# Linear attention and a routed expert layer: the experts' first product with the weights as its stationary side

## Chip, cores and metric

One core of a Trainium2 chip runs the whole kernel in one launch. The metric is the device time in microseconds of that core. Everything is float32.

## The reference, cut to what matters

The input is 2 x 2048 = 4096 tokens of 512 features. The first half of the layer is a linear attention with 16 query heads and 4 key heads of 128, between two normalisations, added back to its input. The second half, which the change is in, is a mixture of 32 experts, of which each token takes 8:

```python
logits = x @ wg.T
scores = softmax(logits)
weights, idx = top_k(scores, 8);  weights = weights / sum(weights)
# the tokens sorted by expert; per expert's group of rows:
g = xs @ w1[e]          # 512 -> 192
u = xs @ v1[e]          # 512 -> 192
h = silu(g) * u
ys = h @ w2[e]          # 192 -> 512
out[t] += ys * weight   # added up over the 8 experts of a token
x + layernorm(out)
```

## The kernel before, in words

**Routing.** While the attention runs, `route_tile` computes the scores of 128 tokens, the place of each token in its experts' lists, and writes token number and weight to `list_d` in DRAM with eight indirect DMAs of GpSimd (L203). `plan_round` (L254 on) cuts the lists into blocks of 128 tokens of one expert. Its tables give, for every block, the token numbers (`tid`), their weights (`wt`), and the expert to load, with a mark where the same buffer still holds that expert's weights (`keep`, L338), in which case the loads are skipped.

**Pairs of blocks.** Two blocks are worked on together, s = 0 and 1. A first round of 24 pairs (L731 to L734) takes blocks that are full after seven of the eight attention tiles; it starts while the last routing work is still going on. A second round of up to 120 pairs follows, cut into parts of 104, 8, 2, 2, 2 and 2 pairs (`PARTS`, L77); each part but the first stands behind a branch on the number of pairs that there really are (L770). In this input 138 pairs run in all: 24, then 104, 8 and 2.

**`prepare`** (L666) takes a pair's buffers `r` (one of three sets, `NR`) and for each of its blocks has SyncE load the expert's first weights (`w1t`, L674: 128 partitions x 4 slices x 384 columns, gate and up side by side) and second weights (`w2t`, L675 and L676), has GpSimd gather the 128 tokens (`xg`, L679), transposes them on TensorE in four 128x128 pieces (`px`, L685), and copies the result to `xgT` on VectorE (L687).

**`run_pair`** (L691) does the two products. For each block, TensorE takes the transposed tokens as the stationary side and streams 384 weight columns against them, in four accumulating steps (`pgu`, L698): the result has tokens on partitions. ScalarE applies silu to the gate half (L701) and VectorE multiplies it with the up half into `hh` (L702), with the 192 features reordered. The two blocks' 2 x 192 features are then transposed in three 128x128 pieces (`ph`, L710) and copied to `hT` (L712): piece 0 holds 128 features of block 0, piece 2 holds 128 of block 1, piece 1 has the remaining 64 of block 0 on partitions 0 to 63 and those of block 1 on 64 to 127. The second product has a full-row part for each block (L715) and a 64-row part for each (L719), which accumulate in `py`. ScalarE scales by the routing weight (L723), and GpSimd adds the rows to `acc_d` in DRAM by an indirect DMA (L724).

**Order.** The Tile framework schedules the instructions of each engine from the program's order and its dependencies; SyncE's order alone is as written. Pools say how many buffers there are: 4 of `xg`, 6 of `xgT`, 2 PSUM tiles each of `px`, `pgu` and `py`, one of `ph`. In the second round the program prepares pair i+1 ahead of running pair i (`second_round`, L752). The pair that stands first behind a branch is prepared in the part ahead of it, into tiles of its own (`ahead`).

A last loop adds up the two accumulators, normalises, and adds the attention's output.

Of the kernel before, what the change touches and what calls it, by code (L numbers as in the profile page):

```python
# [8 lines left out]
F32 = mybir.dt.float32  # L9
I32 = mybir.dt.int32  # L10
U32 = mybir.dt.uint32
AF = mybir.ActivationFunctionType
# [5 lines left out]
P = 128  # L18
# [5 lines left out]
def linear_attention_then_moe(  # L24
# [15 lines left out]
    nc = tc.nc  # L40

    NT, HID = x.shape
# [6 lines left out]
    C = HID // P  # L49
    E = wgT.shape[1]  # L50
    K = 8
    F2 = wgu.shape[1] // C
    F = F2 // 2
    FC = w2r.shape[1] // HID
    FR = F - P
    NR = 3
    NTILE = NT // P
# [15 lines left out]
    NP2 = (NB - N1 + 1) // 2  # L73
# [2 lines left out]

    PARTS = [(NT * K // BS - N1) // 2, 8, 2, 2, 2, 2]  # L77
    assert sum(PARTS) == NP2


    dram = ctx.enter_context(tc.tile_pool(name="dram", bufs=1, space=DRAM))

    x1_d = dram.tile([NT, HID], F32, name="x1_d")
    xn_d = dram.tile([NT + P, HID], F32, name="xn_d")
# [7 lines left out]
    ident = const.tile([P, P], F32, name="ident")  # L92
# [554 lines left out]
    with ExitStack() as mctx:  # L647
        plan = mctx.enter_context(tc.tile_pool(name="plan", bufs=1))
        x1_sb = plan.tile([P, NTILE, HID], F32, name="x1_sb")
# [3 lines left out]
        hp = pairs.enter_context(tc.tile_pool(name="hp", bufs=3))  # L653
        ps_a = pairs.enter_context(tc.tile_pool(name="ps_a", bufs=2, space=PSUM))


        def weights(shape, name):
            return [[wp.tile(shape, F32, name=f"{name}{s}{r}") for r in range(NR)] for s in range(2)]

        w1b = weights([P, C * F2], "w1t")  # L660
        w2b = weights([P, 2, HID], "w2t")

        w2v = w2r.rearrange("r (c h) -> (r c) h", c=FC)
        pairs.enter_context(tc.manual_schedule(engines={mybir.EngineType.SP}))

        def prepare(r, cols, tid, wt, load, xsrc, into=None):  # L666

            xgTs = []
            for s, c0 in enumerate(cols):
                w1t, w2t = w1b[s][r], w2b[s][r]  # L670
                ld = nc.sync.value_load(load[:, c0 : c0 + 1], min_val=0, max_val=2 * E - 1)
                ex = ld & (E - 1)
                skip = {"cond": ld < E, "bounds_check": "skip_entire_dma"}
                nc.sync.dma_start(w1t, wgu[bass.ds(ex * P, P), :], **skip)  # L674
                nc.sync.dma_start(w2t[:, 0, :], w2v[bass.ds(ex * F + s * FR, P), :], **skip)  # L675
                nc.sync.dma_start(w2t[s * FR : (s + 1) * FR, 1, :],  # L676
                                  w2v[bass.ds(ex * F + (1 - s) * P, FR), :], **skip)
                xg = xg_p.tile([P, HID], F32, tag="xg", name="xg")
                nc.gpsimd.indirect_dma_start(  # L679
                    out=xg, out_offset=None, in_=xsrc,  # L680
                    in_offset=bass.IndirectOffsetOnAxis(ap=tid[:, c0 : c0 + 1], axis=0),
                )
                px = ps_a.tile([P, C, P], F32, tag="xt", name="px")
                for c in range(C):
                    nc.tensor.transpose(px[:, c, :], xg[:, c * P : (c + 1) * P], ident)  # L685
                xgT = into[s] if into else hp.tile([P, C, P], F32, tag="xgT", name="xgT", bufs=6)
                nc.vector.tensor_copy(xgT, px)  # L687
                xgTs.append(xgT)
            return xgTs

        def run_pair(r, cols, tid, wt, load, xgTs):  # L691

            hh = hp.tile([P, 2, F], F32, tag="hh", name="hh")
            for s, xgT in enumerate(xgTs):
                w1t = w1b[s][r]
                pgu = ps_a.tile([P, F2], F32, tag="gu", name="pgu")
                for c in range(C):
                    nc.tensor.matmul(pgu, xgT[:, c, :], w1t[:, c * F2 : (c + 1) * F2],  # L698
                                     start=(c == 0), stop=(c == C - 1))
                hs = hp.tile([P, F], F32, tag="hs", name="hs")  # L700
                nc.scalar.activation(hs, pgu[:, :F], AF.Silu)  # L701
                nc.vector.tensor_mul(  # L702
                    hh[:, s, :].rearrange("p (k c) -> p c k", c=FC),
                    hs.rearrange("p (c k) -> p c k", c=FC),
                    pgu[:, F:].rearrange("p (c k) -> p c k", c=FC),
                )
            hf = hh.rearrange("p s f -> p (s f)")
            ph = ps_a.tile([P, 3, P], F32, tag="ht", name="ph", bufs=1)
            for c in range(3):
                nc.tensor.transpose(ph[:, c, :], hf[:, c * P : (c + 1) * P], ident)  # L710
            hT = hp.tile([P, 3, P], F32, tag="hT", name="hT")
            nc.vector.tensor_copy(hT, ph)  # L712
            py = [ps_a.tile([P, HID], F32, tag="y", name=f"py{s}") for s in range(2)]
            for s in range(2):
                nc.tensor.matmul(py[s], hT[:, 2 * s, :], w2b[s][r][:, 0, :],  # L715
                                 start=True, stop=False)
            for s in range(2):
                rows = slice(s * FR, (s + 1) * FR)
                mm = nc.tensor.matmul(py[s], hT[rows, 1, :], w2b[s][r][rows, 1, :],  # L719
                                      start=False, stop=True)  # L720
            for s, c0 in enumerate(cols):
                ysb = hp.tile([P, HID], F32, tag="ysb", name="ysb")
                nc.scalar.activation(ysb, py[s], AF.Copy, scale=wt[:, c0 : c0 + 1])  # L723
                sc = nc.gpsimd.indirect_dma_start(  # L724
                    out=acc_d[s][:, :],
                    out_offset=bass.IndirectOffsetOnAxis(ap=tid[:, c0 : c0 + 1], axis=0),
                    in_=ysb, in_offset=None, compute_op=ALU.add,
                )
            return mm, sc

        done = []  # L731
        for i in range(NP1):
            pair = (i % NR, (i, NP1 + i), *(a[:, 0, :] for a in round1[:3]))
            done.append(run_pair(*pair, prepare(*pair, xn_d[: SNAP * TB, :])))  # L734
# [6 lines left out]
        np2 = plan.tile([P, 1], I32, name="np2")  # L741
        nc.vector.tensor_copy(np2, round2[3])
        np2 = nc.values_load(np2[:1, :], min_val=0, max_val=NP2)

        def pair2(i):
            g, jj = divmod(i, GP2)
            return (NP1 + i) % NR, (jj, GP2 + jj), *(a[:, g, :] for a in round2[:3])


        ahead = [[plan.tile([P, C, P], F32, name=f"ahead{k}{s}") for s in range(2)] for k in range(2)]  # L750

        def second_round(k, ready):  # L752
            i0, n = sum(PARTS[:k]), PARTS[k]
            for i in range(i0, i0 + n):
                if i % 3 == 0 and i // 3 < NTILE:
                    t = i // 3
                    nc.sync.dma_start(x1_sb[:, t, :], x1_d[t * P : (t + 1) * P, :])
                now, ready = ready, None
                if i + 1 < i0 + n:
                    ready = prepare(*pair2(i + 1), xn_d[:, :])  # L760
                elif i + 1 < NP2:
                    ready = prepare(*pair2(i + 1), xn_d[:, :], ahead[k % 2])
                run_pair(*pair2(i), now)
            return ready

        with ExitStack() as asked:
            ready = prepare(*pair2(0), xn_d[:, :])
            for k in range(len(PARTS)):
                if k:
                    asked.enter_context(tc.If(np2 > sum(PARTS[:k])))  # L770
                ready = second_round(k, ready)
        pairs.close()


# [1 line left out]
        for i in range(0, NTILE, 2):  # L776
            rows = slice(i * P, (i + 2) * P)
# [60 lines left out]
```

## Time and profile before

| | |
|---|---|
| median of 3 runs | 2855.76 us (2848.94 to 2856.44) |
| the profiled execution's own time | 2853.38 us |
| its span, first to last instruction | 2851.6 us |
| mean granted TensorE clock | 0.969 |
| first of the experts' products to the last | 1341 to 2763 us |
| DMA moved over the span | 400.35 MB |

A profile is one execution. Each group of instructions is named by its line, engine, operation and tiles, with count, busy time, mean duration, and the idle time of its engine just ahead of it with what ended that. PEld is TensorE's loading of the stationary side, which runs beside its products. A float32 product leaves two records, a transposition one. Matmul durations overlap those of their neighbours, so what one costs is read from the distance of the starts. The slices of section 2 are a fortieth of the span each, 71 us; TensorE is busy for nine tenths or more of nearly all of those between the start and the final stage:

```profile
PE   8999999998999999998769899999999999999850
DVE  5334544546533536564412222222222222222217
POOL 1100223122320122223455455555555555554426
PEclk9999999999999999999889999999999999999985
```

### The profile page before, as it was taken

The page shows a single profiled execution, that of the slowest core. Times are in us where ns is not written, and L with a number is a line of the kernel's source. Part 1 is how long each engine was busy: PE and PEld are TensorE (multiplying, and loading weights), DVE is VectorE, ACT ScalarE, POOL GpSimd, SP SyncE. Part 2 cuts the span into 40 slices and gives each one's busy share as a digit, 9 for nine tenths or more (in the row PEclk, how much of TensorE's full clock was granted, in tenths as well). Part 3 has the DMA queues.
Part 4 walks back from the last instruction along what each step waited for, and adds up shares of the span by engine and source line. Part 5 has one row for each costly group of instructions (what it writes and reads, how often), then busy time and mean ns, then how long its engine had stood idle before and what let it go on. Part 6 is the DMA issues. An engine that isn't in the chain of part 4 may idle for free. (4 is left out here: it accounts for less than half of the span.)

```text
span 2851.6 us, 29678 instructions
## 1 busy us (share of the span) xinstructions
PE 2642.3 (93%) x8451; PEld 1308.6 (46%) x8451; DVE 1062.9 (37%) x2434; ACT 674.9 (24%) x1208; POOL 1062.5 (37%) x893
## 2 busy tenths in 40 slices
PE   8999999998999999998769899999999999999850
PEld 3434444444444444444435455555555555555420
DVE  5334544546533536564412222222222222222217
ACT  4331222313431313121212112121212121212114
POOL 1100223122320122223455455555555555554426
PEclk9999999999999999999889999999999999999985
DMA  3291211212111212123657899989787988676548
GB/s 112 85 327 52 72 52 52 67 52 68 38 56 45 71 34 71 49 75 113 163 113 165 218 268 253 278 201 253 164 215 158 316 195 199 135 193 122 106 89 319
DMA packets 179450, 400.35 MB, mean 140 GB/s; under 512 B 29445, under 2 KB 30470, under 8 KB 178770
## 3 DMA queue, kind: packets, MB, share of 16 engines
q0 software_dynamic: 70304, 145.84, 25.3%
q1 hardware_dynamic: 101602, 237.55, 25.0%
q10 hardware_dynamic: 7376, 15.02, 1.5%
q8 instruction: 70, 1.15, 0.2%
q14 instruction: 98, 0.80, 0.1%
HBM read 491.63 MB, written 116.66 MB: 213 GB/s over the span
## 5 line engine op out<-in xcount | busy, mean ns | idle before, releaser
L698 PE MATMUL pgu<-w1t,xgT 128*128 128x384 f32 x2176 | 767.6, 496 | 3.6 <-issue 2.5
L724 POOL DMA_INDIRECT acc_d<-ysb,tid x276 | 441.5, 1600 | 499.9 <-ACT ysb L723 385.7
L203 POOL DMA_INDIRECT list_d<-tw,pi x256 | 252.6, 987 | 972.0 <-DVE pi L201 556.1
L698 PEld LDWEIGHTS pgu<-w1t,xgT 128*128 128x128 f32 x2176 | 392.9, 191 | 324.3 <-issue 108.6
L552 PE MATMUL pq<-xlT,wq_sb 128*128 128x512 f32 x1024 | 462.0, 597 | 1.2 <-DVE sq L559 1.2
L584 PE MATMUL acc<-m,sq 128*128 128x512 f32 x1024 | 463.0, 597 | 0.0
L702 DVE TENSOR_TENSOR hh<-hs,pgu 128x192 f32<-128x192 f32 x276 | 97.5, 355 | 976.4 <-ACT hs L701 836.2
L723 ACT ACTIVATE ysb<-py,wt 128x512 f32<-128x512 f32 x276 | 176.6, 684 | 786.6 <-PE py L719 738.4
L679 POOL DMA_INDIRECT xg<-xn_d,tid x278 | 276.5, 995 | 119.8 <-PE px L685 68.0
L552 PEld LDWEIGHTS pq<-xlT,wq_sb 128*128 128x128 f32 x1024 | 190.2, 190 | 240.4 <-issue 229.6
L584 PEld LDWEIGHTS acc<-m,sq 128*128 128x128 f32 x1024 | 189.1, 190 | 239.6 <-issue 239.1
L715 PE MATMUL py<-w2t,hT 128*128 128x512 f32 x552 | 266.4, 605 | 2.1 <-issue 2.1
L555 ACT ACTIVATE qe<-pq,nbq_sb 128x512 f32<-128x512 f32 x128 | 87.7, 685 | 512.9 <-PE pq L552 512.9
L559 DVE SCALAR_TENSOR_TENSOR sq<-pq,bq_sb,qe 128x512 f32<-128x512 f32 x128 | 95.7, 748 | 286.4 <-ACT qe L556 286.2
L687 DVE COPY xgT<-px 128x512 f32<-128x512 f32 x272 | 185.5, 683 | 39.9 <-PE px L685 37.4
L685 PE MATMUL px<-ident,xg 128*128 128x128 f32 x1112 | 173.0, 281 | 26.2 <-DMA xg<-xn_d,tid 16.8
L701 ACT ACTIVATE hs<-pgu 128x192 f32<-128x192 f32 x276 | 90.4, 330 | 353.9 <-PE pgu L698 317.1
L685 PEld LDWEIGHTS px<-ident,xg 128*128 128x128 f32 x1112 | 135.1, 145 | 52.8 <-issue 32.4
L715 PEld LDWEIGHTS py<-w2t,hT 128*128 128x128 f32 x552 | 107.5, 196 | 108.8 <-issue 74.2
L719 PE MATMUL py<-w2t,hT 64*128 64x512 f32 x552 | 157.3, 642 | 0.0
L710 PE MATMUL ph<-ident,hh 128*128 128x128 f32 x414 | 100.1, 297 | 46.9 <-DVE hh L702 46.9
L469 PE MATMUL pk<-wk_sb,xlT 128*128 128x512 f32 x256 | 119.6, 607 | 0.0
(188 smaller groups left out, 1868.0 us busy)
## 6 DMA issues: line engine op xcount, KB each, us to landing
w1t<-in_wgu_dram SPq DMA_DIRECT2D x278, 768.0 KB
w2t<-in_w2r_dram SPq DMA_DIRECT2D x278, 256.0 KB
w2t<-in_w2r_dram SPq DMA_DIRECT2D x278, 128.0 KB
nb<-nr_d SPq DMA_DIRECT2D x128, 256.0 KB
acc_d<-zero SPq DMA_DIRECT2D x6, 2048.0 KB
xb<-in_x_dram SPq DMA_DIRECT2D x32, 256.0 KB
xr<-in_x_dram SPq DMA_DIRECT2D x32, 256.0 KB
wo<-in_woT_dram SPq DMA_DIRECT2D x32, 256.0 KB
```

The source lines that it names most:

```text
L203: nc.gpsimd.indirect_dma_start(out=list_d[:, :], out_offset=bass.IndirectOffsetOnAxis(ap=pi[:, k : k + 1], axis=0), in_=tw[:, k, :], in_of ...
L469: nc.tensor.matmul(pk, xlT[:, c, :], wk_sb[:, c, :], start=(c == 0), stop=(c == C - 1))
L552: nc.tensor.matmul(pq, wq_sb[:, c, h * P : (h + 1) * P], xlT[:, c, :], start=(c == 0), stop=(c == C - 1))
L584: nc.tensor.matmul(pa[s], a[:, s * P : (s + 1) * P], ms[h], start=(h == 0), stop=(h == H - 1))
L679: nc.gpsimd.indirect_dma_start(out=xg, out_offset=None, in_=xsrc, in_offset=bass.IndirectOffsetOnAxis(ap=tid[:, c0 : c0 + 1], axis=0),)
L685: nc.tensor.transpose(px[:, c, :], xg[:, c * P : (c + 1) * P], ident)
L687: nc.vector.tensor_copy(xgT, px)
L698: nc.tensor.matmul(pgu, xgT[:, c, :], w1t[:, c * F2 : (c + 1) * F2], start=(c == 0), stop=(c == C - 1))
L715: nc.tensor.matmul(py[s], hT[:, 2 * s, :], w2b[s][r][:, 0, :], start=True, stop=False)
L719: mm = nc.tensor.matmul(py[s], hT[rows, 1, :], w2b[s][r][rows, 1, :], start=False, stop=True)
L723: nc.scalar.activation(ysb, py[s], AF.Copy, scale=wt[:, c0 : c0 + 1])
L724: sc = nc.gpsimd.indirect_dma_start(out=acc_d[s][:, :], out_offset=bass.IndirectOffsetOnAxis(ap=tid[:, c0 : c0 + 1], axis=0), in_=ysb, in_ ...
```

## The change

Four things change, all in the experts' part.

- The first product is turned round. The stationary side is a slice of 128 weight columns, the moving side the transposed tokens: three slices of four accumulating steps, each over 128 tokens. The result has features on partitions, in three slices of one PSUM tile: gate 0 to 127; gate 128 to 191 with up 0 to 63; up 64 to 191.
- Silu is applied to the first two of these slices (256 columns), and four VectorE products a block, of 64, 64, 32 and 32 partitions, write the features straight into `hT`. `hh`, the transposition `ph` and its copy are gone; `pgu` has three PSUM tiles in place of two.
- The features in `hT` stand in another order, so the rows of `w2` are loaded in that order: each of the two loads reads two runs of rows (`two_runs`).
- The second round prepares pairs two ahead of the one that runs, across branches too, as long as a part has more than two pairs. `AHEAD` is 2.

The second product, the scaling and the scatter are as before in the program's text; so is the first round's loop.

```diff
+    AHEAD = 2
...
+        def two_runs(rows, n, p, dc):
+
+            width = FC * HID
+            return bass.AP(rows.tensor, rows.offset, [[p * width + dc * HID, 2], [width, n], [1, HID]],
+                           runtime_checks=rows.runtime_checks)
...
-                nc.sync.dma_start(w2t[:, 0, :], w2v[bass.ds(ex * F + s * FR, P), :], **skip)
-                nc.sync.dma_start(w2t[s * FR : (s + 1) * FR, 1, :],
-                                  w2v[bass.ds(ex * F + (1 - s) * P, FR), :], **skip)
+                first, second = (w2r[bass.ds(ex * FW, FW), c * HID : (c + 1) * HID] for c in range(FC))
+                nc.sync.dma_start(w2t[:, 0, :], two_runs(first, FR, FW - FR, 1), **skip)
+                nc.sync.dma_start(w2t[s * FR : (s + 1) * FR, 1, :], two_runs(second, FR // 2, FR, -1),
+                                  **skip)
...
-            hh = hp.tile([P, 2, F], F32, tag="hh", name="hh")
             for s, xgT in enumerate(xgTs):
-                pgu = ps_a.tile([P, F2], F32, tag="gu", name="pgu")
-                for c in range(C):
-                    nc.tensor.matmul(pgu, xgT[:, c, :], w1t[:, c * F2 : (c + 1) * F2],
-                                     start=(c == 0), stop=(c == C - 1))
-                hs = hp.tile([P, F], F32, tag="hs", name="hs")
-                nc.scalar.activation(hs, pgu[:, :F], AF.Silu)
-                nc.vector.tensor_mul(
-                    hh[:, s, :].rearrange("p (k c) -> p c k", c=FC),
...
-            ph = ps_a.tile([P, 3, P], F32, tag="ht", name="ph", bufs=1)
-            for c in range(3):
-                nc.tensor.transpose(ph[:, c, :], hf[:, c * P : (c + 1) * P], ident)
-            nc.vector.tensor_copy(hT, ph)
+                pgu = ps_a.tile([P, 3, P], F32, tag="gu", name="pgu", bufs=3)
+                w1t = w1b[s][r].rearrange("p (c k f) -> p c k f", c=C, k=3)
+                for k in range(3):
+                    for c in range(C):
+                        nc.tensor.matmul(pgu[:, k, :], w1t[:, c, k, :], xgT[:, c, :],
+                                         start=(c == 0), stop=(c == C - 1))
+                hs = hp.tile([P, 2, P], F32, tag="hs", name="hs")
+                nc.scalar.activation(hs, pgu[:, :2, :], AF.Silu)
+                main, q, t = hT[:, 2 * s, :], FR // 2, s * FR
+                nc.vector.tensor_mul(main[:FR], hs[:FR, 0, :], pgu[FR:, 1, :])
+                nc.vector.tensor_mul(main[FR:], hs[:FR, 1, :], pgu[FR:, 2, :])
+                nc.vector.tensor_mul(hT[t : t + q, 1, :], hs[FR + q :, 0, :], pgu[q:FR, 2, :])
+                nc.vector.tensor_mul(hT[t + q : t + FR, 1, :], hs[FR : FR + q, 0, :], pgu[:q, 2, :])
...
+                prepare_to(i0, i0 + AHEAD)
+                for i in range(i0, i0 + n):
...
+                    prepare_to(i, min(i + AHEAD, i0 + n - 1) + 1)
+                    if i + AHEAD >= i0 + n and n > AHEAD:
+                        j = i + AHEAD
+                        ready[j] = prepare(*pair2(j), xn_d[:, :], ahead[j - i0 - n])
+                    run_pair(*pair2(i), ready.pop(i))
```

More of the change, by code (lines that the diff above doesn't have):

```diff
@@ L78, in linear_attention_then_moe @@
     assert sum(PARTS) == NP2
+    AHEAD = 2
+    assert min(PARTS) >= AHEAD
     dram = ctx.enter_context(tc.tile_pool(name="dram", bufs=1, space=DRAM))
@@ L661, in linear_attention_then_moe @@
         w2b = weights([P, 2, HID], "w2t")
-        w2v = w2r.rearrange("r (c h) -> (r c) h", c=FC)
+        FW = F // FC
+        assert FC == 2 and F == 3 * FR
+        def two_runs(rows, n, p, dc):
+            width = FC * HID
+            return bass.AP(rows.tensor, rows.offset, [[p * width + dc * HID, 2], [width, n], [1, HID]],
+                           runtime_checks=rows.runtime_checks)
         pairs.enter_context(tc.manual_schedule(engines={mybir.EngineType.SP}))
@@ L691, in run_pair @@
         def run_pair(r, cols, tid, wt, load, xgTs):
-            hh = hp.tile([P, 2, F], F32, tag="hh", name="hh")
+            hT = hp.tile([P, 3, P], F32, tag="hT", name="hT")
             for s, xgT in enumerate(xgTs):
-                w1t = w1b[s][r]
-                pgu = ps_a.tile([P, F2], F32, tag="gu", name="pgu")
-                for c in range(C):
-                    nc.tensor.matmul(pgu, xgT[:, c, :], w1t[:, c * F2 : (c + 1) * F2],
-                                     start=(c == 0), stop=(c == C - 1))
-                hs = hp.tile([P, F], F32, tag="hs", name="hs")
-                nc.scalar.activation(hs, pgu[:, :F], AF.Silu)
-                nc.vector.tensor_mul(
-                    hh[:, s, :].rearrange("p (k c) -> p c k", c=FC),
[L704 to L707, printed above, removed]
-            ph = ps_a.tile([P, 3, P], F32, tag="ht", name="ph", bufs=1)
-            for c in range(3):
-                nc.tensor.transpose(ph[:, c, :], hf[:, c * P : (c + 1) * P], ident)
-            hT = hp.tile([P, 3, P], F32, tag="hT", name="hT")
-            nc.vector.tensor_copy(hT, ph)
+                pgu = ps_a.tile([P, 3, P], F32, tag="gu", name="pgu", bufs=3)
[11 more added lines that the diff above has]
+                nc.vector.tensor_mul(hT[t + q : t + FR, 1, :], hs[FR : FR + q, 0, :], pgu[:q, 2, :])
             py = [ps_a.tile([P, HID], F32, tag="y", name=f"py{s}") for s in range(2)]
@@ L747, in pair2, with prepare_to @@
             return (NP1 + i) % NR, (jj, GP2 + jj), *(a[:, g, :] for a in round2[:3])
[L750 to L764, printed above, removed]
+        ahead = [[plan.tile([P, C, P], F32, name=f"ahead{k}{s}") for s in range(2)] for k in range(AHEAD)]
+        ready = {}
+        def prepare_to(i, n):
+            for j in range(i, n):
+                if j not in ready:
+                    ready[j] = prepare(*pair2(j), xn_d[:, :])
         with ExitStack() as asked:
-            ready = prepare(*pair2(0), xn_d[:, :])
-            for k in range(len(PARTS)):
+            for k, n in enumerate(PARTS):
+                i0 = sum(PARTS[:k])
                 if k:
-                    asked.enter_context(tc.If(np2 > sum(PARTS[:k])))
-                ready = second_round(k, ready)
+                    asked.enter_context(tc.If(np2 > i0))
+                prepare_to(i0, i0 + AHEAD)
+                for i in range(i0, i0 + n):
+                    if i % 3 == 0 and i // 3 < NTILE:
+                        t = i // 3
+                        nc.sync.dma_start(x1_sb[:, t, :], x1_d[t * P : (t + 1) * P, :])
+                    prepare_to(i, min(i + AHEAD, i0 + n - 1) + 1)
[3 more added lines that the diff above has]
+                    run_pair(*pair2(i), ready.pop(i))
         pairs.close()
```

## Prediction

> **What bounds the kernel now.** I read the page first: busy shares, the 40 slices, the costliest groups. Then the busy time by stretch, and last TensorE's timeline through one pair of blocks. The change touches only the experts' part, 1341 to 2770 us. In its middle TensorE never rests:
>
> ```profile
> PE 2642.3 (93%) x8451; PEld 1308.6 (46%) x8451; DVE 1062.9 (37%) x2434; ACT 674.9 (24%) x1208; POOL 1062.5 (37%) x893
> ...
> L698 PE MATMUL pgu<-w1t,xgT 128*128 128x384 f32 x2176 | 767.6, 496 | 3.6 <-issue 2.5
> ...
> L710 PE MATMUL ph<-ident,hh 128*128 128x128 f32 x414 | 100.1, 297 | 46.9 <-DVE hh L702 46.9
> ```
> ```profile
> 1663.00:2641.00 978.00, 976.24 (x3596) 529.45 (x3595) 245.99 (x513) 198.38 (x412) 529.24 (x406) 1.00 0.83 208
> ```
>
> The columns of the last line: stretch, its length, busy us of PE, PEld, DVE, ACT, POOL, granted clock, DMA share, GB/s. PE is busy for 976 of 978 us at full clock; every other engine is at 54% or less. So here time is what TensorE issues, and a cost is the distance between starts, not a duration: durations overlap. One pair, TensorE alone (start, duration to the end of the last one, count):
>
> ```profile
> 2019.31 0.27 PE L710 MATMUL ph<-ident,hh 128*128 128x128 f32 x1
> 2019.42 0.93 PE L685 MATMUL px<-ident,xg 128*128 128x128 f32 x7
> 2020.29 0.44 PE L710 MATMUL ph<-ident,hh 128*128 128x128 f32 x2
> 2020.56 0.27 PE L685 MATMUL px<-ident,xg 128*128 128x128 f32 x1
> 2020.67 1.46 PE L698 MATMUL pgu<-w1t,xgT 128*128 128x384 f32 x4
> 2021.96 1.88 PE L715 MATMUL py<-w2t,hT 128*128 128x512 f32 x4
> 2023.77 1.13 PE L719 MATMUL py<-w2t,hT 64*128 64x512 f32 x4
> 2024.83 4.14 PE L698 MATMUL pgu<-w1t,xgT 128*128 128x384 f32 x12
> 2028.81 0.27 PE L710 MATMUL ph<-ident,hh 128*128 128x128 f32 x1
> ```
>
> A float32 product is recorded as two passes, a transposition as one. The pair's period is 2028.81-2019.31 = 9.50 us. By start differences: ph 0.11+0.27 = 0.38; px 0.98, of which 0.10 is the wait for hh (seven at 0.11 are 0.77, not 0.87); pgu 1.29+3.98 = 5.27 (16 passes of 0.323, one of them 0.10 longer, just after the 64-row products); py's full-row part 1.81 (4 x 0.43, and 0.09 before what follows); py's 64-row part 1.06. Sum 9.50. Periods repeat to 0.01 us over a hundred pairs.
>
> **The change, part by part.**
>
> *Features' transposition removed.* ph goes: 3 x 0.11 = 0.33, the hh wait 0.10, and the 0.05 by which ph's last pair exceeds two passes: -0.48 us a pair. Its copy to hT (0.56 us of DVE) goes as well, off the path.
>
> *First product turned round.* 16 passes over 384 columns become 48 over 128, each with its own stationary tile. The trace has such runs, in the key state:
>
> ```profile
> 802.78 0.83 PE L519 MATMUL pc<-ones,sks 128*128 128x128 f32 x6
> ...
> 803.45 3.89 PE L525 MATMUL pg<-gc,wv_sb 128*128 128x128 f32 x32
> ```
>
> L519: (0.83-0.275)/5 = 0.111 us a pass. L525: (3.89-0.275)/31 = 0.117, with two short waits for PSUM in it; starts inside its groups are 0.112 apart. Three at 0.112 are 0.335 against 0.323, so 48 x 0.1117 = 5.36 against 16 x 0.3227 = 5.16: +0.20 us. The ends are 0.109 (px's spacing, -0.13 on the sum) and 0.117 (+0.25). I take 0.112: a block's three slices lie in one PSUM tile, so no wait stands between them.
>
> *The second product's 64-row parts fall apart.* This is not in the diff's text but in the changed program's instruction order. Before, the two 64-row products (rows 0 to 63 for block 0, 64 to 127 for block 1) stand next to each other; the trace starts them 7 ns apart and runs them at once. In the changed program all 144 pairs have main 0, rest 0, main 1, rest 1: no two 64-row products are neighbours. What does a lone one cost? The trace has one pair, in the first round, where routing work came between:
>
> ```profile
> 1374.22 0.60 PE L131 MATMUL pt<-ident,xn 128*128 128x128 f32 x4
> 1374.75 1.12 PE L719 MATMUL py<-w2t,hT 64*128 64x512 f32 x2
> 1375.81 1.08 PE L152 MATMUL pl<-wg_sb,xnT 128*128 128x32 f32 x8
> 1376.81 1.12 PE L719 MATMUL py<-w2t,hT 64*128 64x512 f32 x2
> 1377.87 0.91 PE L698 MATMUL pgu<-w1t,xgT 128*128 128x384 f32 x2
> ```
>
> 1374.75 to 1375.81 and 1376.81 to 1377.87: 1.06 us each, as much as the two together at 2023.77. Around it come 0.09 ahead (start 0.20 after a transposition that takes 0.11) and 0.10 on the first pass behind it, both also around the doubled one. So a lone one is 1.25 us, and two are 2.50 where both cost 1.25 before: +1.25 us a pair.
>
> Here a rule speaks otherwise. The Trainium skill, "TensorE: Matmul & The Clock Gate", section "Why this matters for your kernels", says a matmul with few contraction rows takes the time of a full one and gains only by running beside others. By it a lone one costs a full-row product, 2 x 0.43 = 0.86, and this step +0.47, not +1.25. The row differs because of the 0.1 us at each of four steps; "TensorEngine Tiling (Array Packing)", section "Key Properties", says that changing the tiling mode drains the array, which fits the two outer steps. I take the row. No row has a 512-column full product right behind a lone one; the 0.10 there could be missing (0.02 before pl), which bounds it at -0.2 a pair.
>
> *Silu and products.* ACT works on 256 columns (0.33 us for 192, 0.63 for 512, so about 0.39). DVE does four products a block on 64 or 32 partitions x 128 in place of one of 0.355: between 0.21 and 0.29 each by the slope of its copies (0.56 for 384, 0.68 for 512), at most 0.355 if shifted partitions cost something. DVE goes from 2.6 to some 3.4 us a pair, of 10.5. On the path: block 0's chain lies under block 1's 24 passes (2.68). Block 1's is 0.31 (last pass) +0.39+0.03+4 x 0.29 = 1.9 us, under main 0 and rest 0 (0.86+1.25 = 2.11): nothing. Uncovered it would be 1.9 us a pair.
>
> *Prepared two ahead.* Waits of PE, by semaphores: px waits for its gather. POOL's queue becomes scatter, gather, scatter, gather. By order, the gather of pair 34 stands behind the scatter of pair 30's first block, and its px opens pair 32: about a pair (10 us) for 1.0 us of issue and some 4 of landing. No wait. Weight loads stay tied to the release of one of three buffer sets, three pairs back, so SP issues them at the same point of the pair as before, x1's reload with them. w2's reads become two runs with a stride of 4 KB in place of one contiguous run, still one 2 KB packet a partition (0.084 us median in the packet records): nothing, or, were they doubled, some 0.1 of DMA share on 0.83. xgT of the second round is ready long before its use; there is no wait of pgu there now, so nothing is gained.
>
> *First round.* It isn't prepared ahead, and the order there is px x8 directly ahead of the same pair's pgu. Copying px takes 0.31 after block 0's last transposition, 0.68 and 0.06; behind it only 0.55 of px lies: a wait of 0.50 a pair. The wait of before there is 0.34 (periods of 9.83).
>
> *Boundaries.* Two branches are passed. Before, pgu stops for gathers that only start behind the branch:
>
> ```profile
> 2641.97 1.56 PE L698 MATMUL pgu<-w1t,ahead 128*128 128x384 f32 x4
> 2651.47 1.75 PE L685 MATMUL px<-ident,xg 128*128 128x128 f32 x7 [7.95 <-DMA xg<-xn_d,tid]
> ```
>
> The periods across them are 22.6 and 23.15, so 13.1 and 13.6 us too long (idle, then passes at twice the spacing). After: at the first, px still stands six products into pgu; the last scatter goes out 1.9 us earlier because block 0's result is ready sooner, and 1.34 of pgu hides some: about 9.5 are left, -3.5. At the second, both pairs are ready and the part has no px at all: -13. One pair's preparation that nobody used goes (139 become 138): -1. The last scatter starts about 2 us earlier: -2.
>
> **Sum, against the profiled execution (2853.4; span 2851.6).** A second-round pair: 5.36 + px 8 x 0.109 = 0.87 + mains 1.72 + rests 2.50 = 10.46, +0.96. Over 113 periods +108.5; boundaries and end -19.5. First round: 13 periods of 9.83 become 10.96, +14.7; its first ten pairs take 145 us because POOL's list writes and scatters hold ACT and then PE (idle up to 12.9 us at L710), so most of the addition hides there, +3. Total +107: 2960. The median of the runs (2855.8) lies 2.4 above the profiled one: 2962.
>
> **Rivals.**
> - *The lone 64-row product costs a full-row one (0.86).* Not slower then. For it: the rule. Against: both lone rows. A pair would be 9.68, +0.18: 113 x 0.18 = 20, -19.5, first round +5+1: +7, 2863, no change. It decides from about 0.87 us for each lone product down; below 0.83 the kernel would be faster. 8%, of which 3% for really faster (passes at 0.109 as well: 2847).
> - *Block 1's chain is not covered,* because main 1 waits for all four products and these are slow or queued behind xgT copies. For it: four small operations where one was. Against: 2.11 us of cover and copies that come earlier in the pair. Half a microsecond exposed: 137 x 0.5 = 68, 3030. 6%.
> - *Passes at 0.117, or strided weight reads that make PE wait.* DMA is at 0.83. +30: 2990 to 3000. 9%.
> - The forecast case: 77%, 2930 to 2990 on its own (0.109 to 0.117, the missing 0.10, first round 0 to +35).
>
> **How the numbers follow.** About 0.3%, some 8 us, is what a measurement of this kernel tells from no change. Faster 3%, within 5%, slower 92%. Low end: 2962 - 16 (passes) - 26 (the 0.10 behind a lone product) = 2920. High end: 2990 with the slower passes.
>
> **What would show it.** Steady periods of 10.4 to 10.5 us; pgu starts 0.112 apart; a lone 64-row product 1.06 to the next start with 0.09 ahead; no PE wait at py; first-round periods near 11; the second boundary without idle. Wrong, if the 64-row products stand 0.86 apart, or if the period holds idle time before main 1 or px.

## The result and the profile after

| | before | after |
|---|---|---|
| median | 2855.37 us (2848.94 to 2856.44, 4 runs) | 3322.39 us (3318.25 to 3327.52, 4 runs) |
| span of the profiled execution | 2851.6 us | 3320.9 us |
| mean granted TensorE clock | 0.969 | 0.92 |

The changed kernel takes 1.165 times the time of before (95% interval 1.1634 to 1.1666): 467 us more, where 106 were forecast. The direction was right; the size was not, by 360 us.

The page of the changed kernel, busy shares and three of the costliest groups (L712 is now the first product, L727 the 64-row part of the second, L723 its full-row part):

```profile
PE 2891.8 (87%) x12445; PEld 1703.7 (51%) x12445; DVE 1223.0 (37%) x3122; ACT 706.5 (21%) x1209; POOL 1054.3 (32%) x891
...
L712 PE MATMUL pgu<-xgT,w1t 128*128 128x128 f32 x6432 | 816.9, 291 | 177.5 <-DMA w1t<-in_wgu_dram 172.6
...
L727 PE MATMUL py<-w2t,hT 64*128 64x512 f32 x552 | 336.8, 692 | 65.2 <-DMA w2t<-in_w2r_dram 57.1
...
L723 PE MATMUL py<-w2t,hT 128*128 128x512 f32 x552 | 313.4, 651 | 31.5 <-ACT hs L715 14.4
```

The last column is what there was not before: TensorE stands idle for 172.6 us because w1t has not landed and for 57.1 because w2t has not. Before, no wait for a weight was among the page's costly groups. The same stretch of the second round that showed 976 busy us of 978 before:

```profile
1663.00:2641.00 978.00, 786.72 (x4293) 557.93 (x4292) 241.89 (x673) 143.18 (x267) 346.41 (x271) 0.86 0.61 151
```

TensorE is busy for 787 of 978 us, at a clock of 0.86, and the DMA engines do less, too: their busy share fell from 0.83 to 0.61, their rate from 208 to 151 GB/s. A kernel that waits for data while the DMA engines have more room than before doesn't lack bandwidth in sum; a few of its transfers have too little each. TensorE's timeline shows a pair without a wait and then one with it:

```profile
2187.70 1.02 PE L723 MATMUL py<-w2t,hT 128*128 128x512 f32 x2
2188.65 1.12 PE L727 MATMUL py<-w2t,hT 64*128 64x512 f32 x2
2189.71 1.12 PE L723 MATMUL py<-w2t,hT 128*128 128x512 f32 x2
2190.76 1.12 PE L727 MATMUL py<-w2t,hT 64*128 64x512 f32 x2
2191.82 1.09 PE L696 MATMUL px<-ident,xg 128*128 128x128 f32 x8
2192.74 5.52 PE L712 MATMUL pgu<-xgT,w1t 128*128 128x128 f32 x48
2198.10 1.02 PE L723 MATMUL py<-w2t,hT 128*128 128x512 f32 x2
...
2200.11 1.12 PE L723 MATMUL py<-w2t,hT 128*128 128x512 f32 x2
2204.47 2.04 PE L727 MATMUL py<-w2t,hT 64*128 64x512 f32 x2 [3.23 <-DMA w2t<-in_w2r_dram]
2206.44 1.97 PE L696 MATMUL px<-ident,xg 128*128 128x128 f32 x8
```

From 2187.70 to 2198.10 is a period of 10.40 us, forecast as 10.46, in the forecast order: main, lone 64-row product, main, lone one. Then the 64-row product waits for w2t, and the passes behind the wait take nearly twice as long (px 1.97 in place of 1.09). The granted clock there:

```profile
2206.40:2208.20 1.80, 1.80 (x9) 1.76 (x9) 0.61 (x1) 0.69 (x1) 0.37 (x1) 0.50 0.46 141
```

The clock was 0.50, so each wait costs its length and then slow passes. SyncE's queue in the same stretch (start, duration of the issuing instruction):

```profile
2191.18 1.06 SPq L686 DMA_DIRECT2D w2t<-in_w2r_dram  x1
2192.78 10.01 SPq L687 DMA_DIRECT2D w2t<-in_w2r_dram  x1
2204.43 0.10 SPq L684 DMA_DIRECT2D w1t<-in_wgu_dram  x1
```

The second w2 load (L687) holds the queue for 10.01 us. Over the whole run (count: shortest/median/longest ns, first and last start), before and after:

```profile
L676 SPq DMA_DIRECT2D w2t<-in_w2r_dram x278: 3/147/585, 1333.5 to 2732.9; - x139
L687 SPq DMA_DIRECT2D w2t<-in_w2r_dram x276: 123/138/10502, 1337.3 to 3205.8; - x138
```

The w1t load of the next block stands behind it, which is why most of the idle time is named after w1t, a tile whose own load is unchanged.

The packet records say why. From 1400 us to the final stage, taking SyncE's queue and its 2048-byte packets alone (four in five are w2's, the others are the attention's output `x_sb`, read back for the last stage):

| kernel | packets in flight, mean while any is | mean us of one | packets a us | us for a block's 192 |
|---|---|---|---|---|
| before | 5.38 | 0.0964 | 56 | 3.4 |
| after | 2.11 | 0.0946 | 22 | 8.6 |

A packet takes what it took (median 0.084 us in both); there are only about two at a time. The last two columns are worked out: 2.11 / 0.0946 is 22 a us, and a block's two loads have 128 + 64 packets. A pair in which both blocks change expert then needs 17.2 us for w2 alone, and its period is 10.4.

### The profile page after: what moved, and what is told of

Same layout as the page of the kernel before. It is cut to its first block, busy times and chain, and to the rows that moved or that the text cites. A ratio compares the mean times of both kernels' runs of the same rounds, so it can differ in the third digit from the quotient of the medians.

```text
span 3320.9 us, 38765 instructions
## 1 busy us (share of the span) xinstructions
PE 2891.8 (87%) x12445; PEld 1703.7 (51%) x12445; DVE 1223.0 (37%) x3122; ACT 706.5 (21%) x1209; POOL 1054.3 (32%) x891
## 5 line engine op out<-in xcount | busy, mean ns | idle before, releaser
L712 PE MATMUL pgu<-xgT,w1t 128*128 128x128 f32 x6432 | 816.9, 291 | 177.5 <-DMA w1t<-in_wgu_dram 172.6
L712 PEld LDWEIGHTS pgu<-xgT,w1t 128*128 128x128 f32 x6432 | 799.8, 207 | 189.6 <-issue 159.6
L727 PE MATMUL py<-w2t,hT 64*128 64x512 f32 x552 | 336.8, 692 | 65.2 <-DMA w2t<-in_w2r_dram 57.1
L698 DVE COPY xgT<-px 128x512 f32<-128x512 f32 x268 | 175.5, 687 | 529.2 <-PE px L696 518.8
L717 DVE TENSOR_TENSOR hT<-hs,pgu 64x128 f32<-64x128 f32 x276 | 80.0, 290 | 765.0 <-ACT hs L715 764.7
L723 PE MATMUL py<-w2t,hT 128*128 128x512 f32 x552 | 313.4, 651 | 31.5 <-ACT hs L715 14.4
L731 ACT ACTIVATE ysb<-py,wt 128x512 f32<-128x512 f32 x276 | 190.3, 690 | 584.3 <-PE py L727 517.0
L715 ACT ACTIVATE hs<-pgu 128x256 f32<-128x256 f32 x276 | 105.6, 384 | 978.1 <-PE pgu L712 975.9
L727 PEld LDWEIGHTS py<-w2t,hT 64*128 64x128 f32 x552 | 86.8, 196 | 287.1 <-issue 274.6
L723 PEld LDWEIGHTS py<-w2t,hT 128*128 128x128 f32 x552 | 86.8, 198 | 144.6 <-issue 124.1
```

Of the source, the lines that this page charges most:

```text
L712: nc.tensor.matmul(pgu[:, k, :], w1t[:, c, k, :], xgT[:, c, :], start=(c == 0), stop=(c == C - 1))
```

## The experiments

**Theory.** The new source pattern has two runs as its outermost dimension, and such a load is spread over two of the 16 DMA engines. **Rivals:** preparing two ahead, or SyncE's order, makes loads late; the 4 KB stride is slow by itself; 48 short passes lower the clock.

**Only the loads put back.** In the changed kernel (w2v is the kernel before's view of w2):

```diff
-                nc.sync.dma_start(w2t[:, 0, :], two_runs(first, FR, FW - FR, 1), **skip)
-                nc.sync.dma_start(w2t[s * FR : (s + 1) * FR, 1, :], two_runs(second, FR // 2, FR, -1), **skip)
+                nc.sync.dma_start(w2t[:, 0, :], w2v[bass.ds(ex * F + s * FR, P), :], **skip)
+                nc.sync.dma_start(w2t[s * FR : (s + 1) * FR, 1, :], w2v[bass.ds(ex * F + (1 - s) * P, FR), :], **skip)
```

> The changed kernel with only the kernel before's two w2 loads put back (one contiguous run of rows each); everything else, TensorE's order too, stays as changed. The rows of w2 then do not stand in the order of the features, so the result is another; the amount of work is the same. Theory (a load whose pattern has an outermost dimension of 2 is spread over two of the 16 DMA engines, so w2 comes late and TensorE waits): the waits at py and pgu go, SP's second w2 issue no longer blocks (maximum under 1 us in place of 10.5), and the time is 2940 to 2970, near the 2962 forecast. Rival 1 (preparing two ahead, or the order of SP's queue, makes the loads late): stays near 3322. Rival 2 (the lower clock is TensorE's own load, from 48 short passes): most of the 360 us stay, above 3200.

2948.78 us, 1.0347 of before (1.0329 to 1.0364). The same stretch:

```profile
1663.00:2641.00 978.00, 972.29 (x5967) 690.08 (x5968) 334.06 (x934) 199.41 (x372) 481.77 (x376) 1.00 0.77 196
```

TensorE is busy for 972 of 978 us at full clock, no wait for a weight is left, and the longest w2 issue is 0.91 us. The loads are worth 3322 - 2949 = 373 us. Both rivals with their cause in the rest of the change fall: the rest is still there. The two pages also split it: between the profiled spans lie 371 us (3320.9 less 2950.0); with the same 12445 passes, TensorE is busy for 2891.8 in place of 2772.0 us, so 120 are longer passes, and 251 are more idle time. The clock records agree: TensorE is busy for 300 us at a granted clock of 0.50 in the changed kernel and for 67 us with the loads put back, and half of the difference, 116 us, is what the lower clock adds.

**Only the loads changed.** The same edit the other way round, in the kernel before.

> The kernel before with only the changed kernel's two w2 loads (two runs of rows each); the rows then don't match the features, so the result is another. Theory (two DMA engines for w2): slower by about what the changed kernel lost beyond its forecast, 2855 + 360 = 3215, between 3130 and 3280, with long issues of the second w2 load on SP and waits of py for w2t. Rival 1 (preparing two ahead or the new order is the cause): 2855.

3325.52 us, 1.1667 (1.1636 to 1.1697): above the expectation, and as slow as the whole change. Its waits:

```profile
PE pgu L707 <- DMA w1t<-in_wgu_dram: 282.9, 54, 10.6
PE ph L719 <- DVE hh L711: 45.0, 10, 11.5
PE py L728 <- DMA w2t<-in_w2r_dram: 22.7, 14, 3.9
PE py L724 <- DMA w2t<-in_w2r_dram: 16.1, 7, 3.5
```

The same edit makes 476 us here and 373 in the changed kernel. So the costs do not add: both kernels with two-run loads take the same time (3322 and 3326 us), as if the loads set the pace and the 99 us of TensorE's longer pair lay inside the waits. I had expected 360 because I took the two for a sum.

**Four runs, and sixteen.** Rows stay 4 KB apart within a run, and the outermost dimension changes (first edit: four runs; second: sixteen):

```diff
-            return bass.AP(rows.tensor, rows.offset, [[p * width + dc * HID, 2], [width, n], [1, HID]],
+            return bass.AP(rows.tensor, rows.offset, [[16 * width, 4], [width, 2 * n // 4], [1, HID]],
...
+            return bass.AP(rows.tensor, rows.offset, [[5 * width, 16], [width, 2 * n // 16], [1, HID]],
```

> The changed kernel with w2's source read as four runs of rows in place of two (outermost dimension 4, rows still 4 KB apart, packets still 2 KB, number of loads the same); other rows are read, so the result is another. Theory (engines = outermost dimension): about 4 packets of w2 in flight, a load takes half as long as in the changed kernel, and most of the wait goes: 2960 to 3060. Rival (the 4 KB stride itself slows DRAM reads, whatever the outermost dimension): stays at 3322.

> As the run with four runs of rows, with sixteen (outermost dimension 16, rows still 4 KB apart within a run); other rows are read, so the result is another. Theory (engines = outermost dimension): all 16 engines, no waits left, equal to the run with one contiguous run, 2940 to 2970. Rival (the 4 KB stride itself): stays at 3322.

With four runs 3000.09 us (1.052; 1.0499 to 1.0541), with sixteen 2961.31 (1.0388; 1.0371 to 1.0406).

The first of these is only half the edit that it was meant to be. A block's second load reads 64 rows (n = 32), so its four runs of 16 rows start 16 rows apart: each begins where the one before ends, and together they are a single stretch of 64 rows. Only the first load (n = 64) has four runs that don't join. The page shows it in its count of small packets, here after, with four and with sixteen:

```profile
DMA packets 176530, 400.42 MB, mean 121 GB/s; under 512 B 26613, under 2 KB 27638, under 8 KB 175810
DMA packets 178130, 400.42 MB, mean 134 GB/s; under 512 B 28213, under 2 KB 29238, under 8 KB 177410
DMA packets 179330, 400.43 MB, mean 135 GB/s; under 512 B 29413, under 2 KB 30438, under 8 KB 178610
```

With the loads put back there are 29413 under 512 B as well. In each of these kernels 100 blocks really load weights (the trace has 12800 packets of w1t's 6144 bytes, 128 a load), which is 200 loads of w2. Against the 29413, the changed kernel has 2800 fewer, 14 for each of the 200 loads; the one with four runs has 1200 fewer, 12 for each of 100 loads. That is what is left out if a load leaves one small packet for every engine that it uses, and w2 uses 2 engines in place of 16, or 4 in its first load alone. The packet records of w2's data, as above:

| outermost dimension | packets in flight | packets a us | us for a block's 192 | longest second w2 issue | time |
|---|---|---|---|---|---|
| 2 (after) | 2.11 | 22 | 8.6 | 10.5 us | 3322 |
| 4 (first load), one stretch (second) | 3.73 | 37 | 5.2 | 6.23 us | 3000 |
| 16 | 6.37 | 59 | 3.2 | 0.82 us | 2961 |
| 128 and 64 (only the loads put back) | 6.07 | 62 | 3.1 | 0.91 us | 2949 |

The number in flight rises with the outermost dimension, the stride being the same in the first three rows. The stride as the cause falls. (The runs with four and sixteen read some rows twice; their packets were no shorter for it, 0.102 and 0.108 us in the mean.) With four, two changed blocks need 10.4 us, just the period, and what is left of the loss is 51 us over the run with the loads put back. Of the 12 us between the last two rows some 10 lie in the first round, whose last pair is reached at 1668.9 us in place of 1658.4; why, stays open.

**One ahead again, and two ahead alone.** In the run with the loads put back the second-round loop of before, and in the kernel before the loop of the changed one:

```diff
-                prepare_to(i0, i0 + AHEAD)
...
-                    prepare_to(i, min(i + AHEAD, i0 + n - 1) + 1)
+                if i + 1 < i0 + n:
+                    ready = prepare(*pair2(i + 1), xn_d[:, :])
```

> The changed kernel with the kernel before's w2 loads and the kernel before's second-round loop: pairs are prepared one ahead, not two. The rows of w2 don't match the features, so the result is another. Theory (preparing two ahead pays only where a part ends, 13.1 to 9.5 and 13.6 to 0 us): 15 to 20 us slower than the run with only the loads put back (ratio 1.035 to before), so about 1.041. Rival (preparing two ahead costs something in every pair): not slower, or faster than that run.

> The kernel before with only the second-round loop of the changed kernel: pairs are prepared two ahead. Theory: the two boundaries shrink by 3.5 and 13 us and nothing else moves: 15 to 20 us faster than the kernel before, ratio 0.993 to 0.995. Rival 1 (two ahead delays loads or gathers in every pair): slower, ratio above 1.003. Rival 2 (nothing at the boundaries): 1.00.

2955.88 us (1.0362; 1.0344 to 1.0381), against 1.0347 for the run with two ahead: the intervals overlap, the sign is not told. In the kernel before: 2844.73 us, 0.9977 (0.9967 to 0.9987), 7 us faster, not 17. Steady periods are the same with both loops (10.41; 9.49), so two ahead costs nothing in a pair. In the kernel before it saves 12 us at the second boundary (period 11.05 in place of 23.15) and nearly nothing at the first (22.10 in place of 22.6). And it costs where the second round starts, which neither expectation had. That start with two ahead, in the run with the loads put back:

```profile
1661.55 1.09 PE L688 MATMUL px<-ident,xg 128*128 128x128 f32 x8
1662.99 0.66 PE L688 MATMUL px<-ident,xg 128*128 128x128 f32 x4 [0.35 <-issue]
1663.48 0.39 PE L704 MATMUL pgu<-xgT,w1t 128*128 128x128 f32 x2
1663.70 0.60 PE L688 MATMUL px<-ident,xg 128*128 128x128 f32 x4
1664.14 1.06 PE L704 MATMUL pgu<-xgT,w1t 128*128 128x128 f32 x8
1670.90 1.09 PE L688 MATMUL px<-ident,xg 128*128 128x128 f32 x4 [5.71 <-DMA xg<-xn_d,tid]
```

At 1670.90 TensorE has reached the transposition of a later pair's tokens, which stands in its queue ahead of products that were ready; it waits 5.71 us for the gather, and the passes behind it are slow. The period there is 21.22 us with two ahead and 11.85 with one (in the kernel before 17.15 and 10.53).

**The order written out.** The changed kernel, with four plain loads of w2 (one for each run of rows; w2e is the expert's rows) and, in the second round, TensorE's order as in the program: both first products, the transpositions of the pair two ahead, both full-row parts, both 64-row parts.

```diff
-                nc.sync.dma_start(w2t[:, 0, :], two_runs(first, FR, FW - FR, 1), **skip)
+                nc.sync.dma_start(w2t[:FR, 0, :], w2e[:FR, :HID], **skip)
+                nc.sync.dma_start(w2t[FR:, 0, :], w2e[FW - FR :, HID:], **skip)
...
+            asked.enter_context(tc.manual_schedule(engines={mybir.EngineType.PE}))
```

> The changed kernel with two edits: each run of w2's rows is a load of its own (four loads of 64, 64, 32 and 32 rows in place of two loads of two runs), and in the second round TensorE's order is written out: first products of both blocks, the eight transpositions of the pair two ahead, both full-row second products, both 64-row ones. Theory (loads back on 16 engines, and two neighbouring 64-row products cost 1.25 us, not 2.50): a period of 5.36 + 0.87 + 1.72 + 1.25 = 9.20 us, -0.30 against the kernel before over 113 periods, boundaries -19, first round +20 (there the order is left to the scheduler): 2815, between 2790 and 2850. Rival 1 (the shorter loads cost SP or the queue as much as two-run ones): above 3000. Rival 2 (block 1's silu and products are not covered by the transpositions and the full-row products, 1.73 us): periods of 9.5 to 10, 2850 to 2910.

The second kernel differs from it by the order of two instructions:

```diff
                 nc.tensor.matmul(py[s], hT[:, 2 * s, :], w2b[s][r][:, 0, :], start=True, stop=False)
-            for s in range(2):
                 rows = slice(s * FR, (s + 1) * FR)
```

> The run with the order written out, with one edit: in the second round each 64-row product stands right behind its own block's full-row product (main 0, rest 0, main 1, rest 1), so that no two 64-row products are neighbours. Theory (a lone 64-row product takes 1.25 us with what stands around it, the same as two neighbours): +1.25 us a pair over some 114 pairs, +140 against the run with the order written out. Rival (a lone one costs a full-row product, 0.86): 1.72 in place of 1.25, +0.47 a pair, +54.

Neighbours: 2865.65 us, 1.0045 (1.0028 to 1.0062). Apart: 2978.89, 1.044 (1.0423 to 1.0458). One pair of each, neighbours first:

```profile
2013.61 5.62 PE L715 MATMUL pgu<-xgT,w1t 128*128 128x128 f32 x48
2019.07 1.04 PE L699 MATMUL px<-ident,xg 128*128 128x128 f32 x8
2019.94 1.88 PE L727 MATMUL py<-w2t,hT 128*128 128x512 f32 x4
2021.75 1.13 PE L731 MATMUL py<-w2t,hT 64*128 64x512 f32 x4
2022.81 5.62 PE L715 MATMUL pgu<-xgT,w1t 128*128 128x128 f32 x48
```
```profile
2018.91 5.62 PE L715 MATMUL pgu<-xgT,w1t 128*128 128x128 f32 x48
2024.37 1.04 PE L699 MATMUL px<-ident,xg 128*128 128x128 f32 x8
2025.25 1.02 PE L727 MATMUL py<-w2t,hT 128*128 128x512 f32 x2
2026.20 1.12 PE L730 MATMUL py<-w2t,hT 64*128 64x512 f32 x2
2027.25 1.13 PE L727 MATMUL py<-w2t,hT 128*128 128x512 f32 x2
2028.31 1.12 PE L730 MATMUL py<-w2t,hT 64*128 64x512 f32 x2
2029.36 2.83 PE L715 MATMUL pgu<-xgT,w1t 128*128 128x128 f32 x23
```

2013.61 to 2022.81 is 9.20 us; 2018.91 to 2029.36 is 10.45. The two 64-row products take 1.06 us together as neighbours and 1.05 each apart, with 0.1 lost around each: 1.25 us a pair, as expected. Over 114 pairs that is 142; the runs differ by 113. In the first kernel weights are late again at the shorter period (16.8 us of waits for w1t, none in the second kernel): this stretches five of its periods by 21 us in all.

The first kernel missed its expectation by 51 us. Its steady pairs in the second round have the 9.20 they were given; the 21 us of late weights were not expected. The first round, left to the scheduler, became worse: each block's full-row part directly follows half of the px passes, and its period is 2 x 6.48 = 12.96 us, where 11.02 was the changed kernel's. From its first pair to its last it takes 327 us, 35 more than before, where 20 were expected. The other 15 us or so are not accounted for.

**The order in both rounds.** From the fifth pair on (FREE is 4) the first round is prepared one ahead in the same order, and the second round starts with one pair prepared:

```diff
+                if i == FREE:
+                    late.enter_context(tc.manual_schedule(engines={mybir.EngineType.PE}))
...
-                prepare_to(i0, i0 + AHEAD)
+                if i0 not in ready:
+                    ready[i0] = turn(*prepare(*pair2(i0), xn_d[:, :]))
```

> The run with the order written out in the second round, with two edits: from the fifth pair of the first round on, pairs are prepared one ahead and TensorE's order is written out there too; and the second round starts with one pair prepared instead of two. Theory: the first round's period, 12.96 us in that run (block 1's and block 0's chains both uncovered), comes to 9.21 as in the second round, 19 pairs, -71; the start of the second round gives back the 9 us that the second preparation costs there: 2866 - 80 = 2786, between 2770 and 2830, faster than the kernel before (2850). Rival (the first round's gathers and loads cannot be had earlier, so the periods stay above 11): 2825 to 2860.

2823.0 us, 0.9908 of before (0.9892 to 0.9925): 0.9% faster than before, and 37 us short of the expectation, though inside its range. The first round does reach 9.21, but not in all pairs: around 1440 to 1500 us gathers are late (periods of 16.7 to 19.6), and the round gives back 46 us, not 71. The start of the second round gives back 3 us (12.05 in place of 15.42), not 9. And w1t is late nine times, seven of them in the second round (24.1 of the 25.6 us), where this costs 34 us over 103 periods, 13 more than with the order written out in the second round alone:

```profile
PE pgu L716 <- DMA w1t<-in_wgu_dram: 25.6, 9, 5.1
PE px L700 <- DMA xg<-xn_d,tid: 16.0, 6, 4.0
```

Is the period too short for the loads, or are four loads too many? The last run puts the contiguous loads in:

> The run with the order written out in both rounds, with the kernel before's two w2 loads (one contiguous run each) in place of its four; the rows of w2 then don't match the features, so the result is another. That run has nine waits of the first product for w1t left (25.6 us). Theory A (four loads in place of two cost SP and its queue time): the waits go, and with them the passes at a low clock behind them: 2780 to 2800. Theory B (a period of 9.21 us is simply shorter than a pair's loads take where both experts change): the waits stay and the time with them, 2815 to 2830.

2801.94 us, 0.9828 (0.9811 to 0.9844), 2 us above the first theory's range, and no wait for w1t: the four loads cost 21 us net. The second round says more: 103 of its periods fell from 982.5 to 948.9 us, 34 less, which is 9.21 each. At the start of that round 16 us were lost again (a period of 27.68 in place of 12.05), because TensorE reached tokens that had not been gathered:

```profile
1651.16 1.12 PE L698 MATMUL px<-ident,xg 128*128 128x128 f32 x4 [8.04 <-DMA xg<-xn_d,tid]
```

Why the gather came later there stays open. The packets of the four loads took 0.098 us at the median, those of the two contiguous loads 0.084; whether the number of loads or the 4 KB between rows did it was not separated. A weight layout in DRAM with w2's rows already in the features' order should give about this time with the reference's result; that was not built, so it is not shown.

## Why the prediction was wrong

What was forecast as +106 us was +467. The rest of the change, with the loads put back, was +99 (2948.78 against 2849.57), so the sum for the rest was nearly right, and one term in it was not. That 99 comes so near to 106 is partly luck: three of the parts below came out 4 to 11 us lower than forecast, and one that was not in the sum added 9.

**The step that failed** is this one, in "Prepared two ahead": w2's reads "become two runs with a stride of 4 KB in place of one contiguous run, still one 2 KB packet a partition (0.084 us median in the packet records): nothing, or, were they doubled, some 0.1 of DMA share on 0.83." The packets were as said: 2 KB, 0.084 us. The cost was counted in packets and in the share of all engines, and neither says how many engines one load may use. That was two, and the term was some 370 us (3322.39 against 2948.78), not nothing. A third rival, "strided weight reads that make PE wait", had the mechanism's place, but weighed it by the same DMA share of 0.83 and gave it 30 us. The Trainium skill states the rule, in "DMA: Bandwidth & Descriptors", section "Why a DMA increments its semaphore by 16 and not by 1": the number of engines is the largest one up to 16 that divides the slowest dimension of both access patterns; so 2 for the new loads and 16 for the old. The runs agree with it, by packets in flight (2.1 with two runs, 6.4 with sixteen) and by small packets (2, 4 and 16 a load); which engines carried them the records don't say. Weighed against the trace of before it would have pointed at waits, by an estimate from the page's rule and the trace's packet time: 192 packets of 0.096 us over two engines are 9.2 us a block and 18.5 for a pair that changes both experts, against a period of 10.5.

The other steps, read in the run with the loads put back unless another is named:

- *Features' transposition and first product:* the 48 passes of a pair start over 5.36 us (2192.74 to 2198.10 in the changed kernel), as forecast.
- *Lone 64-row products:* right; 1.25 a pair in a pair of kernels that differ in nothing else. The rival at 0.86 falls.
- *Silu and products covered:* right. Silu took 0.383 us, the four products 0.28 to 0.29 each (forecast 0.39, and 0.21 to 0.29), and steady periods hold no wait.
- *Pair period:* 10.41, forecast 10.46 (its four terms add to 10.45). From the first steady pair to the one ahead of the first boundary, 103 periods are +94.0 (1071.9 against 977.9), forecast 98.9.
- *First round:* period 11.02, forecast 10.96; from its first pair to its last only +7 (299.5 against 292.1), forecast +18. The last 13 periods are +14.2, forecast +14.7; the first ten, under routing work, became 6.8 us shorter where +3 was forecast. Why they did stays open.
- *Boundaries:* from the pair ahead of the first to the last, -10.9 (109.9 against 120.8), forecast -6.9 (ten periods at +0.96 less 16.5). At the first, 7.5 us were left, forecast 9.5; with one ahead it is 8.6, so most of this gain is TensorE's new order and not two ahead. At the second no idle time is left, as forecast.
- *Start of the second round:* not in the sum. The forecast's "No wait" for gathers holds in steady pairs and fails here, where preparing two ahead puts a later pair's gather in front of ready products: 21.22 in place of 11.85, +9.4.

## What to carry to other kernels

Count a changed load's DMA engines before its bytes: with a small outermost dimension, counting packets and bytes ahead of time says that nothing is wrong, while here a block's loads of w2 took nearly three times as long (8.6 us in place of 3.1). The waits can then be named after another tile, whose load stands behind the slow one in the queue (w1t here); look for the issuing instruction that got long. And a preparation that is started earlier also stands earlier in the queue: ask at every start and branch what ready work it is put in front of.

## What was not expected of the hardware

- The issuing instruction of a block's second w2 load held SyncE's queue for up to 10.5 us when both loads had two runs. It held it for up to 6.23 us when only the load ahead of it was confined to four engines and its own was not; with sixteen runs or contiguous loads it took 0.91 us or less.
- Reading as many rows in four loads of 64 and 32 rows, 4 KB apart, in place of two contiguous loads made the median packet 0.098 us in place of 0.084, and cost 34 us over 103 pairs of the second round (21 us of 2823 net).
- After waits of some 3 us the granted clock fell to 0.50. In the changed kernel's experts' part each of TensorE's 35 idle gaps longer than 2.8 us was followed by such a stretch, which began 1.2 to 5.3 us after the gap did and lasted 3.4 us or more. Slower passes were 120 of the 371 us between the two spans. The Trainium skill, "TensorE: Matmul & The Clock Gate", section "Why this matters for your kernels", warns of the half clock after idle gaps above some 3 us, and the trace agrees; the trace of before already showed it at the two boundaries.
